# Perceiver block on one core: half of a value product moved behind the first linear products, weight sums a step later, Exp's table loaded ahead of its use

## The chip, the cores and the metric

The kernel runs on one core of a Trainium2 chip. The metric is the device time of one execution in microseconds (us), lower is better. Before the change it is 615.01 us, the median of 3 runs (614.92 to 615.44).

The core has five engines with a queue of instructions each: TensorE (PE in the profile; its weight loads are listed apart as PEld and overlap the matmuls), VectorE (DVE), ScalarE (ACT), GpSimd (POOL) and SyncE (SP, which here only issues DMAs). An engine runs its queue in order; between engines, instructions wait on semaphores.

## The reference, cut to what matters

All numbers are float32. A batch of 8 sequences of 64 tokens, 512 wide, passes three layers: cross attention onto 1601 context rows per sequence, a block of causal linear attention with an MLP, and a mixture of 8 experts. The change lies at the seam of the first two. Of the second layer this is what counts:

```python
h = _ln(x, g1, beta1)
q = _phi((h @ wq).reshape(b, s, H, DH), proj)      # phi(x) = elu(x @ proj) + 1
k = _phi((h @ wk).reshape(b, s, H, DH), proj)
v = (h @ wv).reshape(b, s, H, DH)
# causal, per head: kv += k_t v_t ; ksum += k_t ; out_t = (q_t kv) / (q_t ksum + 1e-6)
x = x + attn @ wo
```

There are 16 heads of 64, so wq, wk and wv are 512 x 1024.

## The kernel before, in words

**Tiles.** The 512 tokens are 4 tiles of 128 rows (NT = 4; a tile holds two sequences). A width of 512 is 4 blocks of 128 (KC = 4). `h_t` holds h transposed: 128 features of a block on the partitions, 512 tokens along the row.

**Values.** `values(t, n)` (L610) makes half n (512 columns, heads 0 to 7 or 8 to 15) of v for tile t: it opens a PSUM bank, makes one product for each block c (L618), and ACT copies the bank into `v_sb` (L622). In the trace each product of blocks appears as two matmul instructions, so one `values` is 8 of them. The argument `part` picks blocks: the bank is opened with block 0 and copied out after block 3. The calls for the last tile stand at L696 and L697, after everything of the cross attention. The second half of wv lies in a slot of the ring in which the weights stream in (12 slots of 1 MB); the first half lies in a tile that the cross attention's pool holds until L699.

**Queries and keys.** `linear(which, i)` (L756) makes four heads of q or k (256 columns, as two row blocks "even" and "odd" of lin_wq or lin_wk). It saves one product in eight by the scheme of Strassen and Winograd: 7 products of 128 x 256 pieces, each 4 matmul instructions of 256 columns in the trace (all L770), in three PSUM banks, which ACT copies out (L782). POOL adds pieces to one another in place (L786): even and odd receive five such adds, the last of them into odd. A buffer "first" (one buffer) holds the first product; POOL's last add reads it, so the next `linear` may refill it only after that. The second and third product take weight sums, made by `sum_weights(which, i)` (L714): four POOL instructions in a row (L719 to L722), the second of which needs the first, into a tile of four parts with two buffers. `linear` uses the second part first, then the first, and the third and fourth in later products. The sums of tokens that go with them (`hsum_t`) are made before.

The eight calls (L913: query, key, query, key, ...) are called linear 0 to 7 here. Linear 2i and 2i + 1 make the pairs of heads 2i and 2i + 1 (j).

**Features and attention.** `features(j)` (L815) multiplies lin by the 64 x 64 proj (L821: 8 matmul instructions with short rows of 64, into two banks), then ACT makes relu(-x) (L832) from them; the returned `rest` makes Exp on ACT (L836) and adds on DVE (L838), and is called from inside the next `linear`, between its first products. `products(j)` makes the masked products of q and k (L851, DVE L860), `attend_j(j)` sums and value products (L874, L884), `divide` the quotient.

**The order** is written by hand and each engine keeps it. The loop at L917 calls, for j from 0 to 7: linear j; the weight sums for linear j + 2; attention of pair j - 3; products of pair j - 2; features of pair j - 1. The sums for linears 0 and 1 are made ahead of the loop. In POOL's queue the sums stand behind the adds of linear j and ahead of those of linear j + 1.

**ACT's tables.** ACT reads functions from a table set. The set with Sqrt is the one in use up to here; Copy, Identity and Relu run with either. The first Exp of this stage, in linear 2 (L836), has a load of its table ahead of it in ACT's queue, 1.28 us long. Elsewhere the kernel has tiny activations (128 x 1, into a tile warm0 or warm2 that nobody reads), with which a table is loaded at a chosen place.

**Streams.** SP issues the loads of weights in one fixed order, each as soon as a ring slot is free: ..., the second half of wv, the last context rows, wq, wk, wo, then the MLP's w1 and w2, then the experts' weights. `need` and `done` (L212) keep account of slots when the program is built.

Of the kernel before, what the change touches and what calls it, by code (L numbers as in the profile page):

```python
# [16 lines left out]
AF = mybir.ActivationFunctionType  # L17
# [6 lines left out]
NT = B * S // P  # L24
KC = D // P
# [24 lines left out]
def perceiver_kernel(  # L50
# [22 lines left out]
    nc = tc.nc  # L73
# [11 lines left out]
    def mm_bank(name):  # L85
        return ps.tile([P, 512], F32, tag="mm", name=name)
# [121 lines left out]
    def done(*keys):  # L208

        freed.update(keys)  # L210

    def need(*key):  # L212
        if key[0] not in ("ctxT", "ctx", "tail", "wv"):
            done(*[k for k in held if place[k] < place[key] - AHEAD + 1])
            issue_to(place[key] + 1 + AHEAD)
        else:
            issue_to(len(order))
        return streamed[key]
# [16 lines left out]
    for i in range(NIDLE):  # L235
        n = 8 if i < NARROW else P
# [3 lines left out]
    eps = const.tile([P, 1], F32, name="eps")  # L240
# [3 lines left out]
    warm0 = const.tile([P, 1], F32, name="warm0")  # L244
# [332 lines left out]
    def sum_tokens(eng, src, sums, tile):  # L577

        t1, t2, t3, t4 = (ts[:, :, tile * P : (tile + 1) * P] for ts in sums)
        near, far = tokens_of(src, 0, 0, tile), tokens_of(src, 0, 1, tile)  # L580
        eng.tensor_tensor(t1, far, near, ALU.subtract)  # L581
        eng.tensor_tensor(t3, tokens_of(src, 1, 1, tile), far, ALU.subtract)
        eng.tensor_tensor(t2, t3, near, ALU.add)
        eng.tensor_tensor(t4, tokens_of(src, 1, 0, tile), t2, ALU.subtract)
# [25 lines left out]
    def values(t, n, among=lambda: None, part=range(KC)):  # L610
        wv_n = need("wv", n)
        if part[0] == 0:
            v_banks[t, n] = mm_bank(f"v_{n}_{t}")
        bank = v_banks[t, n]
        for c in part:
            if c == KC - 1:
                among()
            nc.tensor.matmul(  # L618
                bank, h_t[:, c, t * P : (t + 1) * P], wv_n[:, c, :], start=(c == 0), stop=(c == KC - 1)
            )  # L620
        if part[-1] == KC - 1:
            nc.scalar.copy(v_sb[:, t, n * 512 : (n + 1) * 512], bank)  # L622
# [70 lines left out]
    values(NT - 2, 0)  # L693
    values(NT - 2, 1, lambda: turn_h(NT - 1))
    sum_tokens(nc.vector, h_t, hsum_t, 1)
    for n in range(2):  # L696
        values(NT - 1, n)  # L697
    done(("wv", 0), ("wv", 1))
    xas.close()  # L699


# [6 lines left out]
    def quarter(which, i, row, half):  # L708

        w = streamed[which, i // 2]  # L710
        at = (2 * (i % 2) + row) * P
        return w[:, 2 * half : 2 * half + 2, at : at + P]

    def sum_weights(which, i):  # L714

        s = wsums[which, i] = sumw.tile([P, 4, 2, P], F32, tag="sumw", name=f"sum_{which}_{i}")
        s1, s2, s3, s4 = (s[:, k] for k in range(4))
        part = lambda row, half: quarter(which, i, row, half)
        nc.gpsimd.tensor_tensor(s1, part(1, 0), part(1, 1), ALU.add)  # L719
        nc.gpsimd.tensor_tensor(s2, s1, part(0, 0), ALU.subtract)  # L720
        nc.gpsimd.tensor_tensor(s3, part(0, 0), part(1, 0), ALU.subtract)
        nc.gpsimd.tensor_tensor(s4, part(0, 1), s2, ALU.subtract)  # L722
# [27 lines left out]
    if True:  # L750
        a_t = la1.tile([P, H * DH // P, B * S], F32, name="a_t")

        nj = H * DH // P
# [61 lines left out]
        def features(j):  # L815

            pr = {which: acc_bank(f"pr_{which}_{j}") for which in ("wq", "wk")}
            for r in range(2):
                rows = slice(r * DH, (r + 1) * DH)
                for which, other in (("wq", r), ("wk", 1 - r)):  # L820
                    nc.tensor.matmul(  # L821
                        pr[which][other * DH : (other + 1) * DH, :],
                        proj2[rows, :],
                        lin[which, j][rows, :],
                        start=True,
                        stop=True,
                    )

            ex = {}
            for which in pr:  # L830
                ex[which] = la2.tile([P, B * S], F32, tag="ex", name=f"ex_{which}_{j}")
                nc.scalar.activation(ex[which], pr[which], AF.Relu, scale=-1.0)  # L832

            def rest(k):
                which = ("wq", "wk")[k]
                nc.scalar.activation(ex[which], ex[which], AF.Exp, scale=-1.0)  # L836
                phi[which, j] = la2.tile([P, B * S], F32, tag=f"phi_{which}", bufs=1, name=f"phi_{which}_{j}")
                nc.vector.scalar_tensor_tensor(phi[which, j], pr[which], 0.0, ex[which], ALU.max, ALU.add)  # L838

            return rest  # L840

        def products(j):


            banks_ = [mm_bank(f"qk_{j}_{r}") for r in range(2)]
            for t in range(NT):
                for h in range(2):
                    cols = slice(t * P + h * S, t * P + (h + 1) * S)
                    for r in range(2):
                        rows = slice(r * DH, (r + 1) * DH)  # L850
                        nc.tensor.matmul(  # L851
                            banks_[r][h * S : (h + 1) * S, t * S : (t + 1) * S],
                            phi["wk", j][rows, cols],
                            phi["wq", j][rows, cols],
                            start=True,
                            stop=True,
                        )
            for r in range(2):
                m = masked[j, r] = la2.tile([P, NT, S], F32, tag="masked", name=f"masked_{j}_{r}")
                nc.vector.tensor_tensor(  # L860
                    m,
                    banks_[r][:, : NT * S].rearrange("p (t q) -> p t q", t=NT),
                    mask[:, None, :].to_broadcast([P, NT, S]),
                    ALU.mult,
                )

        def attend_j(j):

            both = [acc_bank(f"nd_{j}_{h}") for h in range(2)]
            for r in range(2):
                for h in range(2):
                    nc.tensor.matmul(  # L874
                        both[h][r * DH : (r + 1) * DH, NT * S :],
                        ones[h * S : (h + 1) * S, :DH],
                        masked[j, r][h * S : (h + 1) * S, :, :].rearrange("p t q -> p (t q)"),
                        start=True,
                        stop=True,
                    )  # L880
            for t in range(NT):
                for r in range(2):
                    for h in range(2):
                        nc.tensor.matmul(  # L884
                            both[h][r * DH : (r + 1) * DH, t * S : (t + 1) * S],
                            v_sb[h * S : (h + 1) * S, t, (2 * j + r) * DH : (2 * j + r + 1) * DH],
                            masked[j, r][h * S : (h + 1) * S, t, :],
                            start=True,
                            stop=True,
                        )  # L890
            return both

        def denominators(j, both):

            rden = la2.tile([P, 2, NT * S], F32, tag="rden", name=f"rden_{j}")
            for h in range(2):
                nc.scalar.activation(rden[:, h, :], both[h][:, NT * S :], AF.Identity, bias=tiny)  # L897
            return rden

        def divide(j, both, rden=None):  # L900

            if rden is None:
                rden = denominators(j, both)
            nc.vector.reciprocal(rden, rden)  # L904
            for h in range(2):
                nc.vector.tensor_tensor(
                    a_t[:, j, :].rearrange("p (t h q) -> p t h q", t=NT, h=2)[:, :, h, :],
                    both[h][:, : NT * S].rearrange("p (t q) -> p t q", t=NT),
                    rden[:, h, :].rearrange("p (t q) -> p t q", t=NT),
                    ALU.mult,  # L910
                )

        halves_of = [(which, i) for i in range(nj // 2) for which in ("wq", "wk")]  # L913
# [2 lines left out]
        rest = lambda k: None  # L916
        for j in range(nj):  # L917
            linear(*halves_of[j], rest)
            if j + 2 < nj:
                sum_weights(*halves_of[j + 2])  # L920
            if j > 2:
                both = attend_j(j - 3)
                rden = denominators(j - 3, both)
            if j > 1:
                products(j - 2)
            if j > 2:
                divide(j - 3, both, rden)
            if j > 0:
                rest = features(j - 1)
# [1192 lines left out]
```

## Time and profile before

| what | value |
|---|---|
| median of 3 runs | 615.01 us (614.92 to 615.44) |
| the profiled execution | 615.04 us |
| its span, first to last instruction | 613.3 us |
| mean granted TensorE clock | 0.996 of full speed |
| cross attention and values, to the first linear product | 0 to 171.43 us, PE busy 169.88 |
| linear 0 to features 6 | 171.43 to 237.01 us, PE busy 65.45 |
| rest of the linear attention, to the MLP | 237.01 to 268 us, PE busy 30.84 |
| MLP | 268 to about 350 us, PE busy 81.81 |
| experts | about 350 us to the end |

In lines of the timeline the first number is the start and the second the time it took, both in us; then the engine, the line of the program, the operation, output <- inputs by the program's names (buffer numbers left out), sizes, and the number of like instructions put together. A bracket gives the time for which the engine was idle just before and what ended that. "issue" means that nothing was waited for that the profile shows. In the table of windows a line gives the stretch, its length, then for PE, PEld, DVE, ACT and POOL the busy time and the instructions, then the granted clock, the share of the DMA engines and GB/s.

A matmul's shown time overlaps with the next one's; what a matmul costs on PE is the distance from its start to the next start (0.43 us at 512 columns, 0.215 us at 256 columns in this kernel).

### The profile page before, as it was taken

What the parts mean: (1) busy time and instruction counts of PE and PEld (TensorE: products, weight loads), DVE (VectorE), ACT (ScalarE), POOL (GpSimd) and SP (SyncE); (2) the same over time, 40 slices, a digit from 0 to 9 for tenths busy, and PEclk for the clock granted to TensorE, in tenths of its full rate; (3) what the DMA queues carried; (4) which work ended last, traced back from release to release, by engine and by line L of the source; (5) the groups of instructions that cost most, each with busy time, mean ns of one, the idle gap of its engine ahead of it and who ended that gap; (6) DMA issues with size and microseconds to landing.
All of it is one profiled execution on the core that took longest, in us unless ns stands there. A gap on an engine that the chain in (4) does not pass through costs nothing. (4 is left out here: it accounts for less than half of the span.)

```text
span 613.3 us, 9571 instructions
## 1 busy us (share of the span) xinstructions
PE 599.7 (98%) x3820; PEld 394.4 (64%) x3820; DVE 185.7 (30%) x448; ACT 151.2 (25%) x317; POOL 176.1 (29%) x241
## 2 busy tenths in 40 slices
PE   8999999999999999999999999999999999999994
PEld 7543434343477775558888658939763848776793
DVE  4121414234402667865104245412212011101100
ACT  3241313140136665233112311301101101101110
POOL 4000000000188758415996021332300111301111
PEclk9999999999999999999999999999999999999998
DMA  8999999999822003001336414158860778775611
GB/s 333 418 418 421 418 419 415 421 418 409 341 70 69 1 3 138 2 1 34 105 138 261 151 69 149 64 162 320 286 253 1 266 270 292 287 286 179 276 20 17
DMA packets 23942, 131.87 MB, mean 215 GB/s; under 512 B 4372, under 2 KB 4372, under 8 KB 12488
## 3 DMA queue, kind: packets, MB, share of 16 engines
q1 hardware_dynamic: 19496, 122.36, 50.8%
q0 software_dynamic: 3280, 7.61, 5.1%
q10 hardware_dynamic: 1104, 1.07, 0.5%
q8 instruction: 40, 0.66, 0.4%
q14 instruction: 22, 0.18, 0.1%
HBM read 126.08 MB, written 4.94 MB: 214 GB/s over the span
## 5 line engine op out<-in xcount | busy, mean ns | idle before, releaser
L1619 PEld LDWEIGHTS up<-xgT,e_up 128*128 128x128 f32 x896 | 100.7, 192 | 4.5 <-ACT y_sb L1597 2.5
L1619 PE MATMUL up<-xgT,e_up 128*128 128x128 f32 x896 | 101.6, 276 | 1.0 <-PEq L1952 0.6
L1598 POOL DMA_INDIRECT out_dram<-y_sb,dst_late x12 | 18.3, 1526 | 167.8 <-ACT y_sb L1597 97.7
L1585 DVE TENSOR_TENSOR mid<-up,act 128x256 f32<-128x256 f32 x38 | 16.1, 425 | 150.5 <-ACT act L1583 150.5
L1633 PE MATMUL y<-e_wo,mid 128*128 128x512 f32 (+1 forms) x144 | 58.8, 548 | 0.0
L472 PE MATMUL sc<-ctxT,pw_t 128*64 128x401 f32 (+1 forms) x256 | 47.5, 503 | 0.0
L1583 ACT ACTIVATE act<-up 128x256 f32<-128x256 f32 x38 | 14.6, 383 | 119.3 <-PE up L1619 97.1
L533 PE MATMUL av<-ctx,eT 128*64 128x512 f32 x192 | 43.5, 595 | 0.0
L581 POOL TENSOR_TENSOR h_sums<-h_t 128x256 f32<-128x256 f32 x1 | 0.7, 724 | 144.1 <-PE avt L560 144.1
L1633 PEld LDWEIGHTS y<-e_wo,mid 128*128 128x128 f32 x144 | 25.7, 190 | 20.5 <-issue 17.8
L472 PEld LDWEIGHTS sc<-ctxT,pw_t 128*64 128x64 f32 x256 | 18.6, 136 | 27.2 <-issue 24.3
L1042 PE MATMUL side<-v_sb,sum_w 128*128 128x256 f32 x128 | 30.5, 380 | 0.2 <-DVE v_sb L581 0.2
L533 PEld LDWEIGHTS av<-ctx,eT 128*64 128x64 f32 x192 | 13.6, 137 | 25.3 <-issue 24.9
L946 PE MATMUL wo<-wo,a_t 128*128 128x512 f32 x64 | 29.2, 601 | 0.0
L618 PE MATMUL v<-wv,h_t 128*128 128x512 f32 x64 | 29.1, 597 | 0.0
L904 DVE RECIPROCAL rden<-rden 128x512 f32<-128x512 f32 x8 | 26.7, 3343 | 0.2 <-ACT rden L897 0.2
L1042 PEld LDWEIGHTS side<-v_sb,sum_w 128*128 128x128 f32 x128 | 24.2, 190 | 3.9 <-issue 0.6
L1127 PE MATMUL mlp<-w,hid_sb 128*128 128x512 f32 (+1 forms) x50 | 22.3, 584 | 0.0
L480 ACT ACTIVATE scores<-sc,pb 128x401 f32<-128x401 f32 (+1 forms) x16 | 9.5, 591 | 46.6 <-PE sc L472 46.6
L618 PEld LDWEIGHTS v<-wv,h_t 128*128 128x128 f32 x64 | 11.6, 190 | 13.4 <-issue 13.0
L489 DVE TENSOR_REDUCE negmax<-scores 128x1 f32<-128x1601 f32 x4 | 7.3, 1821 | 42.5 <-ACT scores L480 42.5
L946 PEld LDWEIGHTS wo<-wo,a_t 128*128 128x128 f32 x64 | 11.5, 190 | 13.2 <-issue 11.0
(353 smaller groups left out, 917.3 us busy)
## 6 DMA issues: line engine op xcount, KB each, us to landing
e_up<-in_L_ffn_up_dram SPq DMA_DIRECT2D x32, 1024.0 KB, 6.0
ctx<-in_ctx_dram SPq DMA_DIRECT2D x24, 1024.0 KB, 15.7
ctxT<-in_ctx_T_dram SPq DMA_DIRECT2D x24, 802.0 KB, 13.8
e_wo<-in_L_ffn_wo_dram SPq DMA_DIRECT2D x16, 1024.0 KB, 10.1
w<-in_L_attn_w_dram SPq DMA_DIRECT2D x8, 1024.0 KB, 8.3
ctxT<-in_ctx_T_dram SPq DMA_DIRECT2D x8, 796.0 KB, 15.3
wv<-in_L_attn_wv_dram SPq DMA_DIRECT2D x2, 1024.0 KB, 14.0
wq<-in_L_attn_wq_dram SPq DMA_DIRECT2D x2, 1024.0 KB, 15.6
```

The costliest lines, as they stand in the source:

```text
L472: nc.tensor.matmul(sc[h * S : (h + 1) * S, :width], pw_t[:, c, (2 * t + h) * S : (2 * t + h + 1) * S], keys[h][:, c, :], start=(c == 0), s ...
L533: nc.tensor.matmul(av[h * S : (h + 1) * S, :], e_t[:, 4 * g + j, h * S : (h + 1) * S], rows[h][:, j, :], start=(g == 0 and j == 0), stop=F ...
L618: nc.tensor.matmul(bank, h_t[:, c, t * P : (t + 1) * P], wv_n[:, c, :], start=(c == 0), stop=(c == KC - 1))
L904: nc.vector.reciprocal(rden, rden)
L946: nc.tensor.matmul(wo_banks[t], a_t[:, j, t * P : (t + 1) * P], wo_r[j // 4][:, j % 4, :], start=(j == 0), stop=(j == nj - 1),)
L1042: nc.tensor.matmul(bank[:, :HT], weights[:, c, :], rows[:, c, :], start=(first and c == 0), stop=(c == 1), skip_group_check=True,)
L1127: nc.tensor.matmul(acc[t][:, part], hid[:, t * P : (t + 1) * P], w[:, part], start=False, stop=(f == FF // P - 1), skip_group_check=True,)
L1583: nc.scalar.activation(act, bank[:, :FQ], AF.Silu)
L1585: nc.vector.tensor_tensor(hid, bank[:, FQ:], act, ALU.mult)
L1598: nc.gpsimd.indirect_dma_start(out=out, out_offset=bass.IndirectOffsetOnAxis(ap=dst[:n, :], axis=0), in_=y_sb[:n, :], in_offset=None, boun ...
L1619: nc.tensor.matmul(bank[:, m * P : (m + 1) * P], up_of[q][:, c, m * P : (m + 1) * P], xg_t[c], start=(c == 0), stop=(c == KC - 1),)
L1633: nc.tensor.matmul(bank[:, :width], h_t[:, j * P : (j + 1) * P], w[:, 2 * (q % 2) + j, n * width : (n + 1) * width], start=(q + j == 0), s ...
```

## The change

Three edits, all in order alone; what is computed stays the same.

1. Of the last value product, values(3, 1), blocks 0 and 1 stay where they were, ahead of linear 0. Blocks 2 and 3 and ACT's copy of the bank move into the loop, behind linear 1 and ahead of features 0. The ring slot of wv's second half is marked free there. (The call of `need` inside the moved half also lets the builder put three later weight loads into the program there; SP's order of loads is the same.)
2. Behind the moved half, a tiny Exp (128 x 1, into warm0) stands in ACT's queue, ahead of the Relus of features 0.
3. The weight sums for linear j + 1, not j + 2, stand behind linear j, for j from 1 to 6. Behind linear 0 there is none; the sums for linears 0 and 1 still stand ahead of the loop.

```diff
@@ -693,9 +693,9 @@
     values(NT - 2, 0)
     values(NT - 2, 1, lambda: turn_h(NT - 1))
     sum_tokens(nc.vector, h_t, hsum_t, 1)
-    for n in range(2):
-        values(NT - 1, n)
-    done(("wv", 0), ("wv", 1))
+    values(NT - 1, 0)
+    values(NT - 1, 1, part=range(2))
+    done(("wv", 0))
     xas.close()
 
 
@@ -916,8 +916,12 @@
         rest = lambda k: None
         for j in range(nj):
             linear(*halves_of[j], rest)
-            if j + 2 < nj:
-                sum_weights(*halves_of[j + 2])
+            if j == 1:
+                values(NT - 1, 1, part=range(2, KC))
+                done(("wv", 1))
+                nc.scalar.activation(warm0, eps, AF.Exp)
+            if 0 < j < nj - 1:
+                sum_weights(*halves_of[j + 1])
             if j > 2:
                 both = attend_j(j - 3)
                 rden = denominators(j - 3, both)
```

## The prediction

> **What bounds the kernel now.** The page says first that TensorE is the bound, with the other engines under a third of the span:
>
> ```profile
> PE 599.7 (98%) x3820; PEld 394.4 (64%) x3820; DVE 185.7 (30%) x448; ACT 151.2 (25%) x317; POOL 176.1 (29%) x241
> ```
>
> So only PE's holes can be won. The change sits between 168 and 200 us, and I read that stretch stage by stage. In the table of windows the first two columns are the stage and its length:
>
> ```profile
> 171.43:177.47 6.04, 6.04 (x29) 5.33 (x28) 0.00 (x0) 2.82 (x7) 4.83 (x8) 1.00 0.52 174
> ...
> 183.60:185.61 2.01, 2.01 (x9) 0.39 (x8) 0.00 (x0) 0.37 (x1) 2.01 (x4) 1.00 0.00 0
> 185.61:192.25 6.64, 6.51 (x32) 5.15 (x29) 1.38 (x2) 5.44 (x11) 4.89 (x8) 1.00 0.00 0
> 192.25:193.73 1.48, 1.48 (x41) 0.67 (x40) 0.67 (x2) 0.37 (x1) 1.34 (x3) 1.00 0.46 61
> 193.73:199.97 6.24, 6.24 (x32) 5.24 (x28) 1.47 (x3) 4.25 (x10) 5.02 (x8) 1.00 0.39 156
> ```
>
> I call the eight calls of `linear` 0 to 7. Linear 0 takes 6.04 us, linear 3 (behind the short-row features) 6.24, and linears 4 to 7 6.24 each too, but linear 2 takes 6.64: 0.40 too long. Features 0 take 2.01; features 1 take 0.97 (192.76 to 193.73). The granted clock is 1.00 throughout, so these are waits. The timeline names them; the bracket at a weight load is the time for which PE's loader sat idle, and what ended it:
>
> ```profile
> 183.61 0.19 PEld L821 LDWEIGHTS pr_wq<-lin_wq,proj 64*64 64x64 f32 x2 [0.33 <-issue]
> ...
> 184.60 0.13 PEld L821 LDWEIGHTS pr_wk<-lin_wk,proj 64*64 64x64 f32 x1 [0.80 <-POOL lin_wk L786]
> ...
> 187.22 1.28 ACT L836 ACT_TABLE_LOAD   x1
> ...
> 189.46 0.73 PEld L770 LDWEIGHTS wq<-h_sums,sum_wq 128*128 128x128 f32 x4 [0.53 <-ACT lin_wq L782]
> ```
>
> Features 0 wait for POOL's last add into lin_wk. Linear 2 waits for a copy on ACT, which stands behind the table load. POOL itself is late because a weight sum nobody needs yet stands ahead of those adds:
>
> ```profile
> 178.81 0.72 POOL L719 TENSOR_TENSOR sum_wq<-wq 128x256 f32<-128x256 f32 x1
> ...
> 181.66 1.40 POOL L786 TENSOR_TENSOR lin_wk<-lin_wk,first_wk 128x256 f32<-128x256 f32 x2
> ...
> 183.14 1.41 POOL L786 TENSOR_TENSOR lin_wk<-lin_wk,part_wk 128x256 f32<-128x256 f32 x2
> ...
> 192.80 0.73 POOL L786 TENSOR_TENSOR lin_wq<-lin_wq,first_wq 128x256 f32<-128x256 f32 x1
> ...
> 193.49 0.73 POOL L719 TENSOR_TENSOR sum_wq<-wq 128x256 f32<-128x256 f32 x1
> ...
> 194.29 0.73 POOL L720 TENSOR_TENSOR sum_wq<-sum_wq,wq 128x256 f32<-128x256 f32 x1
> ...
> 194.49 1.70 PEld L770 LDWEIGHTS wk<-h_sums,sum_wk 128*128 128x128 f32 x8
> ```
>
> The last four lines matter for the cost: in linear 3 the first loads of sum_wk come at 194.49, while POOL is at the second part of the sum that it began behind linear 2.
>
> **Part 1: half of the value product moves.** values(3, 1) is 8 matmuls, one each 0.43 us (168.00 to 171.43). Four move, 4 x 0.43 = 1.72 us. PE's work is the same; linear 0 starts at 171.43 - 1.72 = 169.71 and linear 1 ends at 183.51 - 1.72 = 181.79. Can linear 0 start so early? It loads the second sum of sum_wq 0.65 us after its start, at 170.36; POOL has it at 169.11 + 0.72 = 169.83. Its third and fourth sums (170.51, 171.19) are loaded after 172.9. POOL finishes sum_wk at 174.03 and only then does linear 0's adds, so linear 0's last add ends near 177.6, and ACT's first copy in linear 1 (one buffer, it waits for that add) starts 1.8 us after linear 1's start where it is 1.4 now (178.88 - 177.47). PE needs that copy 2.6 us after the start: covered by 0.4 us.
>
> The four matmuls then fill 181.79 to 183.51. With no weight sum between, POOL makes lin_wk's adds as ACT delivers: the last part copy ends 5.81 us after linear 1's start (182.91 + 0.37 - 177.47), at 181.56, and its add near 182.35. Features 0 start near 183.6 without a wait and take 0.97 as features 1 do, not 2.01: **-1.03 us**. If the cover fell away, PE would wait until 182.35 + 0.06, 0.5 us after linear 1's end.
>
> The PSUM bank of values(3, 1) stays open over linears 0 and 1, which have three banks instead of four. Linear 1 opens its second and third at about 176.6 and 177.5; linear 0's copies leave them at 175.5 and 176.3. I take nothing; the bounds are nothing and, were a bank handed out one place later, the 0.4 us to the next copy. A sum left open with other banks' matmuls between is nothing new: `linear` does that with all of its banks.
>
> Queues: the extra copy on ACT (0.59) goes from 171.63, where ACT was idle, to 183.72, where it idled 1.66 us. On SP, wv's ring slot comes free 12 us later. A w load waits for it and issues at 171.63 now; it would issue at 183.7 and the one behind it waits for linear 2 anyway (192.38). None lands where anyone needs it before 268, when the MLP starts. Nothing.
>
> **Part 2: Exp's table.** The load (1.28) leaves 187.22, where the copy for linear 2 stood behind it, and follows the moved copy: copy 183.72 to 184.31, load to 185.61, the tiny Exp (0.20 in such rows, with the next instruction 0.11 after its start), first Relu at 185.73, as now (185.75). Two Relus and linear 2's first copy keep their spacing, 1.09 and 0.37: the copy ends near 187.2. PE, in linear 2 since 184.58, wants it 2.70 after its start (linear 3: 193.73 to 196.43), at 187.28. The next copies fall at 188.1 and 188.9 against wishes at 188.14 and 189.0. So the 0.40 goes, but with 0.05 to 0.1 to spare, and I charge 0.05 back: **-0.35 us**. ACT's rows say what a load costs its queue:
>
> ```profile
> 133.09 0.58 ACT L622 COPY v_sb<-v 128x512 f32<-128x512 f32 x1 [5.16 <-PE v L618]
> 133.70 1.28 ACT L688 ACT_TABLE_LOAD   x1
> 134.99 0.20 ACT L688 ACTIVATE warm<-eps 128x1 f32<-128x1 f32 x1
> ```
>
> The load begins 0.03 us after a copy like ours. [...]
>
> **Part 3: the sums come a step later.** The same six sums stand in the loop; POOL's order changes from "sum for j+2 behind linear j" to "sum for j+1 behind linear j", so each is needed one linear earlier. Measured from the end of a linear's matmuls (192.15 for linear 2), POOL's last add starts 0.65 later, and the second sum ends 2.87 later (194.29 + 0.73 - 192.15). The next linear's load of that sum comes:
> - linear 2: after the four value matmuls and features, with POOL done early: sum ready near 184.65, wanted at 185.35. Covered.
> - linear 3: after products and features only, 2.34 after linear 2's end (194.49). The sum is 2.87, and PE's answer to POOL takes 0.06 (adds end 184.54, load 184.60): 0.59 late for the load. A load that waited runs beside its matmul at only about 0.1 us extra instead of its usual 0.2 ahead, so PE loses about **+0.50 us**.
> - linears 4 to 7: attend comes between; load 3.28 after the end (203.16 - 199.88) against 2.87 + 0.06. Covered by 0.35.
>
> No row shows a wait of PE for a sum; the bounds of that cost are nothing if POOL runs 0.6 earlier, and 1.96 if PE waits for all four sums (fourth ends at 196.39, 4.24 after the end). Which? At 163.70 a values matmul runs on h_t while DVE writes other columns of h_t from 163.91 to 165.27, so waits go by part of a tile. I take the second sum.
>
> **Sum:** -1.03 - 0.35 + 0.50 = -0.88 us. Behind linear 3 every order is as before and PE has no DMA wait after 160 us in the list of waits, so the shift should arrive whole at the end. The profiled execution took 615.04, its span 613.3 and 1.74 around it; 615.04 - 0.88 = 614.16, and the median shown (615.01) is 0.03 lower: 614.1 us, 0.14% less. About 0.2% (1.23 us) is what a measurement of this kernel can tell from no change.
>
> **The rivals.**
> 1. Forecast: features' wait and the table's gone, one new wait in linear 3. 613.8 to 614.5. Chance 0.55, of which 0.05 reaches past 0.2%.
> 2. The new wait doesn't come: POOL's adds in linear 2 end sooner, as ACT is free earlier. -1.38 to -1.43: 613.6. Against it: POOL's last add follows PE's last product, whatever was ahead. 0.13.
> 3. [...] 0.13.
> 4. It ends elsewhere inside: the 0.35 of cover in linears 4 to 7 doesn't hold by 0.1 to 0.3 each, four times: 614.5 to 615.4. 0.12.
> 5. Slower: PE waits for the fourth sum, not the second. It decides once the wait exceeds the cover: linear 0 loses 0.9, linear 2 0.7, linear 3 2.0 and linears 4 to 7 about 1.0 each (4.24 + 0.06 - 3.28), 7.6 in all, less the 1.4 won: +6.2, 621.2 us. Against it: h_t above. 0.07.
>
> Faster: 0.13 + 0.05 = 0.18; slower 0.07; the rest 0.75. The range takes in rivals 1 to 4: 613.5 to 615.5.
>
> **What would show it.** Right: weight loads of pr_wk without a POOL bracket; linear 2 at 6.24 and features 0 near 1.0 long; the load of the table near 184.3; in linear 3 a bracket of about 0.8 with POOL sum_wk, and linear 3 near 6.7. Wrong: such a bracket in linears 4 to 7, a hole between table load and Relu, or a wait of linear 1 for a bank.

## The result, and the profile after

The changed kernel takes **615.88 us** (median of 22 runs, 615.00 to 618.04) where the kernel before takes 615.02 (22 runs, 614.74 to 615.61). The ratio is 1.0015, 95% interval 1.0009 to 1.0021: 0.9 us slower, where 0.9 us faster was forecast, and outside the forecast's range of 613.5 to 615.5. The profiled execution took 616.74 with a span of 615.0 (613.3 before).

First the stretch that was changed. The stages of the changed kernel in the table of windows, in order: the four moved matmuls, features 0, linear 2, linear 3 (the row of the stage ahead of linear 3 is left out).

```profile
182.22:184.03 1.81, 1.81 (x6) 0.57 (x4) 0.00 (x0) 0.37 (x1) 1.73 (x3) 1.00 0.00 0
184.03:185.05 1.02, 1.02 (x10) 0.21 (x9) 0.00 (x0) 0.91 (x2) 0.94 (x3) 1.00 0.00 0
185.05:191.29 6.24, 6.24 (x33) 5.24 (x29) 1.38 (x2) 5.00 (x12) 3.88 (x7) 1.00 0.49 168
...
192.77:199.49 6.72, 6.51 (x33) 5.16 (x29) 1.47 (x3) 4.34 (x10) 5.07 (x8) 1.00 0.36 143
```

Features 0 are 1.02 long instead of 2.01, linear 2 is 6.24 instead of 6.64, linear 3 is 6.72 instead of 6.24. These are the three terms of the forecast's sum, -1.0, -0.4 and +0.5, as they stood in it. The timeline of the changed kernel names the new wait and shows the table load at its new place:

```profile
184.13 0.59 ACT L622 COPY v_sb<-v 128x512 f32<-128x512 f32 x1 [1.34 <-PE v L618]
...
184.72 1.28 ACT L922 ACT_TABLE_LOAD   x1
...
186.02 0.20 ACT L922 ACTIVATE warm<-eps 128x1 f32<-128x1 f32 x1
186.13 0.58 ACT L832 ACTIVATE ex_wq<-pr_wq 128x512 f32<-128x512 f32 x1
...
193.33 0.72 POOL L720 TENSOR_TENSOR sum_wk<-sum_wk,wk 128x256 f32<-128x256 f32 x1
...
194.11 1.59 PEld L770 LDWEIGHTS wk<-h_sums,sum_wk 128*128 128x128 f32 x8 [0.61 <-POOL sum_wk L720]
```

The second sum ends at 194.05, and PE loads it at 194.11 without waiting for the third and fourth (to 195.43). Up to linear 3 the changed kernel has won about 1 us.

Now the rest. Setting each PE matmul beside the same matmul of the kernel before, the difference stays at -0.45 to -0.59 us from linear 3 to 528 us (the profiled execution had begun 0.4 us late, at its very first transposes), and then it jumps to +1.48 at one place in the expert stage. PE's timeline there, in the changed kernel:

```profile
527.76 1.02 PE L1637 MATMUL y<-e_wo,mid 128*128 128x512 f32 x2
530.58 1.98 PE L1637 MATMUL y<-e_wo,mid 128*128 128x512 f32 x4 [1.79 <-issue]
```

The kernel before runs the six y matmuls in one go:

```profile
528.25 2.74 PE L1633 MATMUL y<-e_wo,mid 128*128 128x512 f32 x6
```

"issue" says that PE waited for nothing that the profile shows, neither a transfer of data nor another engine. What stands just ahead is a conditional branch of PE's sequencer, of which the expert stage has several: does expert e have tokens beyond its first tile? In the view of the branch's line, cut to 515 to 530 us, the columns after the name are the shortest, median and longest duration in ns. The changed kernel, then the kernel before:

```profile
L1960 PEldq COMPARE_BRANCH  x1: 5128/5128/5128, 522.0 to 522.0; - x1
```

```profile
L1956 PEldq COMPARE_BRANCH  x1: 1037/1037/1037, 522.6 to 522.6; - x1
```

The view of the DMA queues has rows for the fetching of code ("instruction"); q8 moves 40 pieces of 16 KB in an execution of either kernel. From 515 us to the start of this branch (522.6), the kernel before fetches one such piece:

```profile
q1 hardware_dynamic: 388, 2.80, 88.9%
...
q8 instruction: 1, 0.02, 0.8%
```

The changed kernel has none from 515 up to 524.7, though its branch began at 522.0:

```profile
q1 hardware_dynamic: 471, 3.34, 82.4%
...
q14 instruction: 1, 0.01, 0.2%
```

In the raw records the pieces start at 521.20 and 525.53 before, and at 524.74 and 527.87 after. So in the changed kernel PE's code came late (that q8 carries it is inferred, at the end of the experiments). The wait at the branch, to 527.13, is itself hidden but for about 0.1 us: ten y matmuls and four transposes that stand ahead of it run on to 527.24, and the transposes behind it start at 527.30 (527.75 before; the four ahead of it start at 526.82, and at 527.39 before). What PE loses is the hole 13 instructions behind the branch (21 from the first of the eight transposes, the "some 20" of the expectations below), which ends at 530.58, behind the second of the late pieces (527.87).

And the changed kernel's code does lie elsewhere. Its trace has 7818 instructions on PE (matmuls, weight loads, waits, branches), the one before 7813: five wait instructions more, 145 against 140, all in the linear attention. In the views of the lines, after:

```profile
L770 PEldq EVENT_SEMAPHORE  x28: 51/51/1772, 165.8 to 231.0; - x28
```

and before 18 at L770; L821 has 6 instead of 11. Everything behind stands 5 places further on.

### The profile page after: what moved, and what is told of

Read it like the earlier page. It is cut to its first block, busy times and chain, and to the rows that moved or that the text cites. A ratio compares the mean times of both kernels' runs of the same rounds, so it can differ in the third digit from the quotient of the medians.

```text
span 615.0 us, 9575 instructions
## 1 busy us (share of the span) xinstructions
PE 598.0 (97%) x3820; PEld 392.4 (64%) x3820; DVE 185.9 (30%) x448; ACT 151.3 (25%) x318; POOL 176.3 (29%) x241
```

## The experiments

**Is it the place of the code?** Theory P: the five extra PE instructions move the branch and its target against the 16 KB pieces in which code is fetched. Rival T: the branch is late because the weights' transfers around it run 0.6 us earlier than before. The small idle matmuls at the very start, which multiply the identity by itself while PE waits for its first data, move all later code by 4 places each and touch nothing else (in the trace each is two weight loads and two matmuls).

The changed kernel with one idle matmul fewer (now 1 place behind):

```diff
-NIDLE = 23
-NARROW = 13
+NIDLE = 22
+NARROW = 12
```

> The changed kernel with one of the small idle matmuls at the very start left out (22 instead of 23; 4 instructions fewer on PE, no work of the computation). Its instructions of the expert stage then stand 1 place behind those of the kernel before, where the change alone has them 5 behind. Theory P (the 5 extra waits on PE move the expert stage's branch against the blocks in which PE's code is fetched): the branch near 522 us takes about 1 us again, and the time falls from 615.9 to about 614.1 to 614.3. Theory T (the branch is late because the transfers around it run at another moment): nothing changes, 615.9.

Measured: **613.87 us**, beside 614.89 for the kernel before on the same chip; ratio 0.9985, 95% interval 0.9976 to 0.9994. That is -1.02 us, where the forecast's sum for the whole change was -0.88. The branch and the hole behind it, in this kernel:

```profile
L1960 PEldq COMPARE_BRANCH  x1: 1104/1104/1104, 521.6 to 521.6; - x1
```

```profile
527.26 2.74 PE L1637 MATMUL y<-e_wo,mid 128*128 128x512 f32 x6
```

Four instructions that compute nothing, half a millisecond ahead of the branch, bring the branch back to 1.1 us and close the hole. Theory P said so; T is out: this kernel reaches the branch even earlier (521.6) than the changed kernel does (522.0; before 522.6), and the branch is quick.

The changed kernel with two idle matmuls fewer (3 places ahead of before; NIDLE = 21, NARROW = 11):

> The changed kernel with two of the small idle matmuls at the start left out (21; 8 instructions fewer on PE): the expert stage stands 3 places ahead of where the kernel before has it. Theory P: 614.1 to 614.3 if the border of a block lies between 0 and 5 places, and no other branch comes to a border. Theory T: 615.9.

Measured: 614.15 us, ratio 0.9989 (0.9980 to 0.9998), branch 1.24 us. Quick again.

The kernel before with one more idle matmul (4 places behind; NIDLE = 24, NARROW = 14):

> The kernel before with one more small idle matmul at the start (24; 4 more instructions on PE): the expert stage stands 4 places behind. Theory P: if the border lies at 4 places or fewer, the branch near 522 us takes about 5 us and the time rises to 616.5 to 617; if it lies at 5, 615.0. Theory T: 615.0.

Measured: 614.81 us, ratio 1.0001 (0.9992 to 1.0010), branch 0.88 us. Four places are harmless.

The kernel before with two more (8 places behind; NIDLE = 25, NARROW = 15):

> The kernel before with two more small idle matmuls at the start (25; 8 more instructions on PE), past the 5 places of the change: theory P expects the late branch, 616.5 to 617, with nothing of the change in it. Theory T: 615.0.

Measured: **616.47 us**, ratio 1.0030 (1.0018 to 1.0043). Nothing of the change is in this kernel, and it has the changed kernel's branch and its hole at the same matmul:

```profile
L1956 PEldq COMPARE_BRANCH  x1: 4669/4669/4669, 522.2 to 522.2; - x1
```

```profile
527.87 1.02 PE L1633 MATMUL y<-e_wo,mid 128*128 128x512 f32 x2
529.86 1.99 PE L1633 MATMUL y<-e_wo,mid 128*128 128x512 f32 x4 [0.96 <-issue]
```

So the loss belongs to the place, and the border lies between 4 and 8 places.

**The parts, each alone**, with programs 1, 3, 0 and 4 PE instructions longer than before, all on the quick side.

Only the half value product moved:

```diff
-    for n in range(2):
-        values(NT - 1, n)
-    done(("wv", 0), ("wv", 1))
+    values(NT - 1, 0)
+    values(NT - 1, 1, part=range(2))
+    done(("wv", 0))
...
+            if j == 1:
+                values(NT - 1, 1, part=range(2, KC))
+                done(("wv", 1))
             if j + 2 < nj:
```

> Of the change, only the move of half of values(3, 1); sums and table load stay as before. PE's program is 1 instruction longer, on the safe side of the border. Working of the prediction: the four matmuls fill the wait of features 0, -1.0 us, and linear 2's wait for the copy behind the table load (0.4) stays: about 613.9 where the kernel before is at 614.9. Rival (POOL's sum between the adds still holds features 0 up): -0.3 to -0.6.

Measured: 613.83 us beside 614.93, ratio 0.9984 (0.9975 to 0.9993): -1.1 us. Features 0 are 1.01 long, linear 2 still 6.64, with the old wait for the table:

```profile
188.49 0.73 PEld L770 LDWEIGHTS wq<-h_sums,sum_wq 128*128 128x128 f32 x4 [0.53 <-ACT lin_wq L782]
```

The move needs neither of the other two parts: POOL's sum between the adds costs nothing once four matmuls stand in the hole.

Only the sums a step later:

```diff
-            if j + 2 < nj:
-                sum_weights(*halves_of[j + 2])
+            if 0 < j < nj - 1:
+                sum_weights(*halves_of[j + 1])
```

> Of the change, only the sums that come a step later. 3 instructions more on PE, on the safe side. Working of the prediction: features 0 wait 0.45 less, as POOL has no sum between linear 0 and linear 1; linear 2's first sum is late by some 0.5, of which the wait for the table load hides a part; linear 3 waits 0.5: +0.1 to +0.5 in all, 615.0 to 615.4. Rival (POOL's order costs nothing): -0.45.

Measured: 615.02 us, ratio 1.0000 (0.9991 to 1.0009): +0.1, at the lower end of what was expected. All three terms are in the timeline of weight loads; the first answers to 184.60 in the kernel before:

```profile
184.19 0.13 PEld L821 LDWEIGHTS pr_wk<-lin_wk,proj 64*64 64x64 f32 x1 [0.34 <-POOL lin_wk L786]
...
186.49 1.59 PEld L770 LDWEIGHTS wq<-h_sums,sum_wq 128*128 128x128 f32 x8 [0.56 <-POOL sum_wq L720]
...
194.72 1.59 PEld L770 LDWEIGHTS wk<-h_sums,sum_wk 128*128 128x128 f32 x8 [0.61 <-POOL sum_wk L720]
```

Features 0 start 0.41 earlier; linear 2 waits for its sum, which takes the place of most of its wait for the table (6.70 long, 6.64 before); linear 3 is 6.71. This part of the change gains nothing by itself and costs 0.5 us in linear 3.

Only the tiny Exp, behind linear 1:

```diff
+            if j == 1:
+                nc.scalar.activation(warm0, eps, AF.Exp)
             if j + 2 < nj:
```

> Of the change, only the tiny Exp, behind linear 1 in ACT's queue. PE's program is as long as before. Working of the prediction: ACT idles 1.66 us ahead of the Relus and the load takes 1.28, so linear 2's wait of 0.4 goes: -0.4 us, 614.5. [...]

Measured: 614.41 us, ratio 0.9992 (0.9983 to 1.0001); the interval just reaches 1, the size is the expected one (-0.5). In ACT's timeline the load follows the copy by 0.02 us and the Relu waits for features 0, not for the load:

```profile
183.50 0.37 ACT L782 COPY lin_wk<-wk 128x256 f32<-128x256 f32 x1 [0.44 <-PE wk L770]
183.89 1.28 ACT L920 ACT_TABLE_LOAD   x1
...
185.53 0.60 ACT L832 ACTIVATE ex_wq<-pr_wq 128x512 f32<-128x512 f32 x1
```

Linear 2 is 6.24 long: the whole 0.40 is gone.

**A version without the give-back.** The change, but with the sums for linears 2 and 3 both behind linear 1, and from then on two linears ahead as before:

```diff
-            if 0 < j < nj - 1:
-                sum_weights(*halves_of[j + 1])
+                sum_weights(*halves_of[2])
+            if 0 < j and j + 2 < nj:
+                sum_weights(*halves_of[j + 2])
```

> The whole change, but behind linear 1 POOL makes the sums for linear 2 and linear 3, and from then on those for linear j + 2 behind linear j as before. PE's program is 4 instructions longer than before, the largest length that was still quick. If linear 3's wait for its sum is the 0.5 us that the change gave back: -1.4 us, 613.5, and below the changed kernel with four instructions fewer by 0.4 to 0.5. Rival (the double sum holds up linear 2's adds and so features or products): no gain over that kernel.

Measured: **613.43 us** beside 614.93; ratio 0.9975, 95% interval 0.9966 to 0.9984: -1.5 us. Linears 2 and 3 both have their bare length:

```profile
184.62:190.86 6.24, 6.24 (x33) 5.24 (x29) 1.39 (x2) 5.00 (x12) 6.08 (x10) 1.00 0.48 168
192.34:198.58 6.24, 6.24 (x32) 5.24 (x28) 1.47 (x3) 4.25 (x10) 5.28 (x9) 1.00 0.39 152
```

It beats the kernel before and the changed one, and its program is 4 PE instructions longer than before, one short of the border. It lies 0.44 below the changed kernel at 1 place; the two intervals overlap, so that step rests on the trace: linear 3 takes 6.24 here and 6.71 there.

**The border, and how wide the slow stretch is.** The kernel with only the half value product moved, shifted by one idle matmul to exactly 5 places (NIDLE = 24, NARROW = 14):

> The kernel with only the half value product moved, and one more small idle matmul at the start: its expert stage stands 5 places behind that of the kernel before, exactly as in the changed kernel, but with other waits. Theory P (the place alone decides, the border lies between 4 and 5): the branch near 522 us takes about 4 to 5 us and the time goes from 613.8 to 615.3 to 615.9. Theory W (the five waits of the change matter, not their number): 613.8.

Measured: 615.85 us (615.07 to 617.88), 2.0 above the same kernel at 1 place; branch 5.29 us. The place alone decides, and the border lies between 4 and 5.

The kernel before, 16 and 32 places behind (NIDLE = 27 and 31, NARROW = 17 and 21):

> The kernel before with four more small idle matmuls at the start: 16 places behind. How wide is the slow stretch? If the late branch comes from a target that lies just ahead of the end of a block of code, it should go on until the target itself lies in the next block. With the hole after some 20 instructions at 5 places, 16 places should still be slow: 616 to 617. Rival (only a few places are slow): 614.9.

> The kernel before with eight more small idle matmuls at the start: 32 places behind, past the 20 or so instructions that ran between target and hole. If the reading of the hole is right, the target then lies in the next block: one fetch instead of two, 614.9 to 615.6. Rival (the fetch of the target is what costs, not the second one): still 616 to 617.

Measured: 617.04 us (ratio 1.0031, 1.0019 to 1.0043) and 618.25 us (1.0059, 1.0037 to 1.0081), branches 4.90 and 4.09 us. The second expectation fell: 32 places are no relief but worse, with both pieces of code still fetched late and the hole now inside the transposes:

```profile
530.47 0.60 PE L1573 MATMUL xgt<-ident,xg 128*128 128x128 f32 x4 [2.29 <-issue]
```

My reading that the stretch ends once the target has left its piece was wrong. What the raw records of all thirteen kernels, before and after among them, say is plainer. In the eight kernels at places -3 to 4 a 16 KB piece of code starts between 520.1 and 521.5, ahead of the branch, and the next between 524.1 and 525.6. In the five at places 5, 5, 8, 16 and 32 the first starts only at 524.4 to 525.1, while the branch is waiting, and a second one 3.1 to 3.4 us later. What sets off the early fetch up to place 4, and where the slow stretch ends, stays open. One candidate was not tested: PE has a BRANCH_PREFETCH_HINT (the kernel's `hint_ahead`, L1962 in the kernel before) 5.1 us ahead of this branch (517.44 to 522.58 in the kernel before), in every one of the kernels. Up to place 4 the early piece starts 3.6 to 4.1 us after the hint (at 521.20 in the kernel before); from place 5 on no piece starts between hint and branch, so in these five the hint alone did not bring the code.

The queue's records don't name their engine. That q8 carries PE's code is inferred, from two things: from place 5 on the branch ends 2.4 to 2.5 us after its piece starts, and in the code from 16 to 381 us PE runs 255 instructions per piece on average (4338 over 17 pieces in the kernel before), while no other engine has over 560 in the whole trace.

## Why the prediction was wrong

Point by point, by its own steps.

**Part 1, -1.03:** right. 2.01 to 1.02 in the changed kernel, and alone 1.1 us of the time. The bracket that should have vanished at pr_wk is still printed at pr_wq (0.76, POOL lin_wk), but it is the loader's idle time, and PE itself has no hole over 0.1 us there: the last moved matmul starts at 183.51 and its 0.43 ends at 183.94, features start at 184.03. One reading was off without harm: in the kernel before, features 0 wait not for POOL's last add into lin_wk (184.51 to 185.23, for the other pair of heads) but for the one ahead of it, which ends at 184.55; the sum used that time. The open bank cost nothing: linear 1 is 6.05 long (176.17 to 182.22 in the table of windows).

**Part 2, -0.35:** right; linear 2 fell to 6.24. Copy, load, tiny Exp and Relu follow each other without a gap: the load takes 1.28, from the end of the copy at 184.72 to 186.00, the Exp starts at 186.02 and the Relu at 186.13. The forecast's upper end, 615.5, and its chance of 0.13 for a slower load or Exp rest on up to 1.4 us more than the rows; no run shows that term. With the tiny Exp alone the load took 1.28 too (183.89 to 185.17), with the Exp at 185.18.

**Part 3, +0.50:** right in place, size and cause: linear 3 is 0.48 longer, PE waits for the second sum and not for the fourth, and linears 4 to 7 have no such wait in the list. The bracket is 0.61 where I said 0.8.

**The sum, -0.88:** measured as -1.02 once the code lies 1 place from where it lay.

**The step that failed** is the one behind the sum: "Behind linear 3 every order is as before and PE has no DMA wait after 160 us in the list of waits, so the shift should arrive whole at the end." The order was as before, and no data was late. But I counted the change's PE work as unchanged because it has the same matmuls, and never asked what its new waits do to the length of PE's program. They made it 5 instructions longer, the kernel before stood less than 5 from a place where the code behind one branch of the expert stage comes late, and that cost about 1.9 us (from 1.02 faster than the kernel before to 0.86 slower), nearly twice the gain. None of the rivals had it; they all looked for the loss inside the linear attention.

The rows that could have warned stood in the trace of before. The list of PE's waits, from which the step took that there is no DMA wait, has PE waiting twice for a branch of its own sequencer (PEq), for 0.3 us (L2006) and for 0.6 us here:

```profile
PE up L1619 <- PEq L1952: 0.6, 1, 0.6
```

And the same branch line on PE took from 82 to 4430 ns:

```profile
L1956 PEldq COMPARE_BRANCH  x6: 82/100/4430, 402.1 to 544.7; - x6
```

Four of the six (82 to 101 ns) run on into the block behind them, whose own branch (L1950) is PE's next one, within 0.2 us. Two jump past that block, at 429 us (4430 ns, hidden under matmuls that were queued ahead) and at 522 us (1037 ns). So a jump of over 4 us was in the kernel already, and the shifted kernels show that the one at 522 us was quick only by the place of its code.

Where PE's code goes on without a branch, the trace shows no such loss: from 171 to 237 us, where five pieces are fetched in the kernel before, PE is busy for 65.45 of 65.58 us. Behind the jump the two pieces were hidden up to 4 places and cost 1.6 to 3.3 us from 5 on.

## What to carry to other kernels

In this kernel with branches, a change of order at 168 to 200 us altered the time at 528 us by 1.9 us, by shifting code: before believing or discarding a difference of a microsecond or two in such a kernel, run the same kernel with a few idle instructions more or fewer at the start, and compare the durations of the branches. When a wait is filled with moved work, check alone which parts of the change carry the gain; here the moved half product alone gave 1.1 us, as much as the three parts together, as the "later" sums gave back what the table load had won (0.4 to 0.5 us) until the one that was due too soon was put back. Measure a sum's lateness against the first load that needs it, not against the start of the stage: that term came out within 0.02 us.

## What the runs showed of the hardware that was not expected

- One conditional branch on PE takes 0.9 to 1.4 us or 4.1 to 5.3 us depending on a shift of a single instruction place (4 or 5) half a millisecond into a program of which PE runs over 7800 instructions. The loss is 1.9 to 2.0 us at 5 places, 1.6 at 8, 2.1 at 16 and 3.3 at 32.
- The kernels from place 5 on also scatter more: 615.00 to 618.04 for the changed kernel and 615.07 to 617.88 for the other one at 5 places, against 614.74 to 615.61 for the kernel before. Queue q1 alone, with the experts' weights, takes 82 to 89% of the DMA engines' time in that stretch (the views above), and the views count the code's queue on the same 16 engines; that this is the reason is argued, not shown.
- The change of order lengthened PE's program (the sums alone by 3 instructions, the moved product alone by 1, the tiny Exp alone by none): its rows have 145 wait instructions instead of 140 (at L770 0.05 us in the median; linear 2 has its bare 6.24 with them).
